# Layer 1 of a four-layer graph network: groups of 6, 7, 6, 6 blocks, a second bank for small products, and twelve blocks of features made earlier

## The chip, the cores and the metric

The kernel runs on one NeuronCore of a Trainium2 chip. A core has a matrix engine (TensorE, "PE" in the profile, with its weight loads as "PEld"), a vector engine (VectorE, DVE), a scalar engine (ScalarE, ACT), a general engine (GpSimd, POOL) and a queue that issues transfers (SyncE, SP). Each engine works through its own instructions in order and waits on semaphores for the others. Matrix products are written to PSUM, which this program uses as eight banks of 128 x 512 fp32 values. Everything else lies in SBUF or in device memory (HBM).

The metric is the time of one execution in microseconds on the device. A profile is one execution with the profiler on; its span runs from the first instruction to the last.

## What is computed

The input is a graph of 3125 nodes with 128 features each and 103125 edges, sorted by destination. Four layers follow each other, each with a residual and a normalisation over the features:

```python
edge_index = jnp.stack([src, dst])
x = _layernorm(x + _L0_gnn_ref(x, src, dst, edge_weight, ...))   # relu(A_w (x W) + b)
x = _layernorm(x + _L1_gnn_ref(x, edge_index, ...))              # attention with 4 heads
x = _layernorm(x + _L2_gnn_ref(x, Wq, Wk, Wv, Wo, edge_index))   # attention with one head
x = _layernorm(x + _L3_gnn_ref(x, edge_index, ...))              # two mean aggregations, sigmoid
```

Layer 1, where the change lies, is graph attention with four heads of 32 channels:

```python
h = (x @ W).reshape(n, HEADS, C)
a_s = jnp.einsum('nhc,hc->nh', h, att_src)
a_d = jnp.einsum('nhc,hc->nh', h, att_dst)
e = jax.nn.leaky_relu(a_s[src] + a_d[dst], NEG_SLOPE)
m = jax.ops.segment_max(e, dst, num_segments=n)
p = jnp.exp(e - m[dst])
z = jax.ops.segment_sum(p, dst, num_segments=n)
alpha = p / (z[dst] + EPS_SOFTMAX)
out = jax.ops.segment_sum(h[src] * alpha[:, :, None], dst, num_segments=n)
out = out.reshape(n, HEADS * C) + gat_bias + x @ skip_W + skip_b
# then a normalisation over the features with gain ln_g and offset ln_b
```

## The kernel before

**Dense instead of sparse.** The 3125 nodes are padded to 25 blocks of 128. At its start the kernel builds from the edge list two dense 3200 x 3200 matrices in device memory: the number of edges between each pair of nodes (`f_ctd`, in bf16), and the sum of their weights (`wd`, fp32). From then on each layer is a sum of matrix products over these.

**Layer 0** multiplies `wd` with the features (`add0`, L801). Twenty of its blocks are accumulated during the building. The last five are accumulated in a tail, a loop over 25 source blocks `i` (L1191). While PE does these, the first work of layer 1 for the finished twenty blocks is hooked into the tail: their attention scores (`scores1`, with `marks` at i = 3 to 6), the copy of the scores out of PSUM (`heads`, called in `top` at i = 7), exponentials of them (`factors`, i = 9), and the features themselves (`values`, two blocks a call, at i = 13, 16, 19 and 22, so eight blocks).

**Layer 1** uses that exp of a leaky relu is one of two products of a source factor and a destination factor, and which of them is right depends only on the sign of a_s + a_d. So for each head there is a mask of 128 sources by some destinations: the edge counts where the sign is positive, 0 elsewhere. Products of the counts and of the masks with scaled features (in three bf16 parts, `vp`) give sums for all destinations.

The work is a list of steps `items` (L1229): over the groups `IG` of destination blocks, over two passes per group (heads 0 and 1, then heads 2 and 3), over 25 source blocks `c`. A step does two things:
- `masks` (L1233), two steps ahead of their use: a transfer `ct` of counts, and for each of the two heads a mask `cm`. In four of five masks ACT makes `fm` (L1255) and DVE takes a minimum with the counts (L1256); in one of five DVE does it alone (L1249). The width of all of these is the group's: 128 columns a block. At the start of a pass a transfer `adr` brings the destinations' scores.
- `products` (L1260), three matrix products for each block of the group: one with the counts (L1266) and two with the masks (L1271). Each block of the group owns one PSUM bank through a pass.

At the end of a pass DVE reduces the banks (`sums`, L1290), POOL combines the parts (L1296 to L1299), and some steps later `quotients` divides (L1306 to L1312). After the second pass `finish1` (L1039) takes over: a normalisation, the gain, offset and residual on POOL (L1052 to L1054), a second normalisation, and then for each block a turn (`turn2`: transpose at L1014, a product with layer 2's weights at L1018). These small products, and the skip products of `skips` (L1279, added by DVE at L1280), use a PSUM bank that `bank()` hands out.

**Delays.** `later(k, f)` runs `f` k steps on (L955); `step()` does what is due. So `quotients` come 4 steps after a pass's end, `finish1` 3 steps after the second quotients, the second normalisation 5 steps after the first, and turns follow every two steps. The order within an engine is made by the framework's scheduler: it takes instructions by program order, but one that it believes ready can go ahead of one that it believes waiting. What it arranged is seen in the trace.

**Banks.** In group 0 layer 0's banks are still in use: five called acc0 to acc4, two called left0 and left1, and one called tr_sa for the small scores. Four of them (acc3, acc4, left0, left1) hold group 0's sums; acc0 and acc1 serve `values` by turns, acc1 also serves as `few`, and acc2 serves `scores1` of the last blocks, which are due at steps 3 and 5; `heads` and `factors` of those blocks come at step 7. From group 1 on there are seven banks acc1_0 to acc1_6 for sums and one bank `few` for small products. `values` of the remaining blocks are made in group 0's first pass, two blocks at a time, four steps before their use.

Of the kernel before, what the change touches and what calls it, by code (L numbers as in the profile page):

```python
# [7 lines left out]
F32 = mybir.dt.float32  # L8
# [7 lines left out]
P = 128  # L16
N = 3125
NB = 25
# [11 lines left out]
H, C = 4, 32  # L30
# [467 lines left out]
Z0 = 20  # L498
# [1 line left out]
GA = 80.0  # L500
UP = 2.0**60
GM = 40.0
IG = [(0, 4), (4, 7), (11, 7), (18, 7)]
QG = [(0, 13), (13, 12)]
LN = N - (NB - 1) * P
GT = [(0, 4), (4, 4), (8, 4), (12, 4), (16, 4), (20, 2), (22, 2), (24, 1)]
# [4 lines left out]
def fast_path(  # L511
# [4 lines left out]
    nc = tc.nc  # L516
# [50 lines left out]
    zps = zero.enter_context(tc.tile_pool(name="f_zps", bufs=1, space=PSUM))  # L567
# [164 lines left out]
    watt = cst.tile([P, 2 * H], F32, name="watt")  # L732
# [138 lines left out]
    acc0 = None  # L871
# [63 lines left out]
    def turned(ps, xT, b0, n, tag="tr"):  # L935

        t = ps.tile([P, 512], F32, name="tr", tag=tag)
        for k in range(n):
            nc.tensor.transpose(t[:, k * P : (k + 1) * P], x[:, b0 + k, :], ident)
        copy(xT[:, b0 * P : (b0 + n) * P], t[:, : n * P])  # L940
# [3 lines left out]
    xT = lp.tile([P, NP], F32, name="f_xT")  # L944
# [10 lines left out]
    def later(k, f):  # L955
        due.append((now[0] + k, f))
# [123 lines left out]
    with ExitStack() as st:  # L1080
# [29 lines left out]
        def scores1(g):  # L1110

            b0, n = GB[g]
            tag = f"acc{min(g, 2)}"
            turned(zps, xT, b0, n, tag)
            for k in range(n):
                b = b0 + k
                nc.tensor.matmul(
                    t8[:, b * 2 * H : (b + 1) * 2 * H], xT[:, b * P : (b + 1) * P], watt, start=True, stop=True
                )
            t = zps.tile([P, 512], F32, name="tr_ad", tag=tag)  # L1120
            nc.tensor.matmul(t[0:H, : n * P], watt[:, H:], xT[:, b0 * P : (b0 + n) * P], start=True, stop=True)
            ad = fp.tile([H, 512], F32, name="ad", bufs=1)
            nc.scalar.copy(ad[:, : n * P], t[0:H, : n * P])
            nc.sync.dma_start(add_[:, b0 * P : (b0 + n) * P], ad[:, : n * P])

        def heads(b0, n):

            b = slice(b0, b0 + n)
            nc.vector.tensor_copy(
                sa[:, b, :], t8[:, b0 * 2 * H : (b0 + n) * 2 * H].rearrange("p (b h) -> p b h", h=2 * H)  # L1130
            )
            nc.vector.tensor_scalar(nas[:, b], sa[:, b, 0:H], -1.0, None, OP.mult)
            nc.gpsimd.tensor_scalar(bas[:, b], sa[:, b, 0:H], UP, None, OP.mult)

# [45 lines left out]
        keep = {}  # L1180

        def top():
            heads(0, Z0)
            ex = fp.tile([P, H], F32, name="ex", bufs=1)
            nc.vector.tensor_reduce(ex, sa[:, 0:Z0, 0:H].rearrange("p b h -> p h b"), AX.X, OP.max)
            keep["d"] = highest(fp, ex, H)
# [4 lines left out]
        for i in range(NB):  # L1191
            add0(tp, i, acc1, (Z0, NB - Z0))
            if i in marks:
                marks[i]()
            if i >= 13 and i % 3 == 1:
                values(ready)
                ready += 2
        tail.close()
# [5 lines left out]
            end0(acc1[g], b0, n)  # L1204
        later(3, lambda: scores1(Z0 // 4))
        later(5, lambda: scores1(Z0 // 4 + 1))
        later(7, lambda: (heads(Z0, NB - Z0), factors(Z0, NB - Z0)))

        def in_range():

# [73 lines left out]
        def sums(acc, g, hp):  # L1284

            i0, n = IG[g]
            pool = lp if (g, hp) == (len(IG) - 1, H - 2) else sp
            nz = pool.tile([P, 7, 2, PW], F32, name="nz")[:, 0:n]
            for k in range(n):
                nc.vector.tensor_reduce(  # L1290
                    nz[:, k], acc[k][:, 0 : 2 * HW].rearrange("p (h s c) -> p h c s", s=3, c=PW), AX.X, OP.add
                )
            hi = nz[:, :, :, 0:F1]
            lo = nz[:, :, :, F1 : 2 * F1]
            fbb = [fb[:, s, i0 : i0 + n, hp : hp + 2, None].to_broadcast([P, n, 2, F1]) for s in range(2)]
            nc.gpsimd.tensor_tensor(lo, lo, fbb[1], OP.mult)  # L1296
            nc.gpsimd.tensor_tensor(hi, hi, fbb[0], OP.mult)
            nc.gpsimd.tensor_tensor(hi, hi, lo, OP.add)
            nc.gpsimd.tensor_tensor(hi, hi, self_[:, i0 : i0 + n, hp : hp + 2, :], OP.add)  # L1299
            if hp == 0:  # L1300
                nc.gpsimd.tensor_copy(deg[:, i0 : i0 + n], nz[:, :, 0, 2 * F1])
            last = pool is lp

            def quotients():
                rz = pool.tile([P, 7, 2], F32, name="rz")[:, 0:n]
                nc.vector.tensor_scalar(rz, hi[:, :, :, C], 1e-38, None, OP.max)  # L1306
                nc.vector.reciprocal(rz, rz)
                nc.gpsimd.tensor_tensor(
                    hi[:, :, :, 0:C], hi[:, :, :, 0:C], rz[:, :, :, None].to_broadcast([P, n, 2, C]), OP.mult
                )  # L1310
                rh = r[:, i0 : i0 + n, hp * C : (hp + 2) * C].rearrange("p b (h c) -> p b h c", c=C)
                nc.gpsimd.tensor_tensor(rh, rh, hi[:, :, :, 0:C], OP.add)  # L1312
                if hp == H - 2:
                    later(1 if last else 3, lambda: finish1(ends[-1], g, (1, 1) if last else (1, 5)))

            later(1 if last else 4, quotients)

        ends.append(sp)
        acc = None
        for x_, (g, hp, c) in enumerate(items):  # L1320
            i0, n = IG[g]
            if (g, hp, c) == (1, 0, 0):
                zero.close()
                ap = st.enter_context(tc.tile_pool(name="f_ap1", bufs=1, space=PSUM))
                spare.append(lambda: ap.tile([P, 512], F32, name="few"))
            if c == 0:
                if g == 0:
                    acc = [zps.tile([P, 512], F32, name="acc1", tag=f"acc{3 + k}") for k in range(2)]
                    acc += [zpp.tile([P, 512], F32, name="acc1", tag=f"left{k}") for k in range(2)]
                else:  # L1330
                    acc = [ap.tile([P, 512], F32, name=f"acc1_{k}") for k in range(n)]
            if c == (2 if g else 0) and hp == (0 if g else H - 2):
                later(0, lambda: skips(i0, i0 + n))
            if (g, hp, c) == (0, 2, 5):
                later(0, in_range)
            step()
            if g == 0 and hp == 0 and ready < NB and ready <= c + 4:
                values(ready)
                ready += 2
            for y_ in range(x_ if x_ == 0 else x_ + 2, min(x_ + 3, len(items))):  # L1340
                masks(*items[y_])
            if c < NB - 2:
                for k in range(n):
                    products(acc, g, hp, c, k)
            elif c == NB - 1:
                for k in range(n):
                    products(acc, g, hp, NB - 2, k)
                    products(acc, g, hp, NB - 1, k)
                sums(acc, g, hp)
# [397 lines left out]
```

## Time and profile before

| | us |
|---|---|
| median of 3 runs | 1522.51 (1521.67 to 1522.7) |
| profiled execution, time | 1520.03 |
| profiled execution, span | 1518.2 |
| PE busy | 1386.5 (91%) |
| PE weight loads busy | 1214.1 (80%) |
| DVE busy | 979.0 (64%) |
| ACT busy | 905.9 (60%) |
| POOL busy | 129.9 (9%) |
| first product of layer 1 | at 543.6 |
| last product of layer 1 | ends at 957.3 |

How to read it: a busy share is over the whole span, which here is a front (the matrices are built), layer 0's tail, and layers 1 to 3, each limited by something else. A row of the profile names a line of the kernel, the engine, the operation, what it writes and reads, and its shape; then busy time, the mean of one instruction in ns, and the idle time of the engine just before such instructions with what ended it. A matrix product's duration includes its way through the array, so products overlap; their pace is seen from start to start. In layer 1 a step of 7 blocks has 21 products.

### The profile page before, as it was taken

The numbers are of one execution on the slowest core, as the hardware profiler recorded it, in microseconds if no ns is written. First come the engines' busy times: TensorE is split into PE (matmuls) and PEld (weight loads), VectorE is DVE, ScalarE is ACT, GpSimd is POOL, SyncE is SP. The second block draws the span as 40 slices with busy tenths as digits, with TensorE's granted clock in tenths as the row PEclk, the third lists the DMA queues.
The fourth block names the chain that finished last, engine by engine and source line by source line (L and its number), as shares of the span: only waits on it lengthen the run. The fifth ranks groups of instructions, "written<-read, shape, count | busy, mean of one in ns | idle before, by whom it ended". The sixth has DMA issues, their size and how long they took to land. (4 is left out here: it accounts for less than half of the span.)

```text
span 1518.2 us, 35039 instructions
## 1 busy us (share of the span) xinstructions
PE 1386.5 (91%) x14762; PEld 1214.1 (80%) x14775; DVE 979.0 (64%) x1619; ACT 905.9 (60%) x1847; POOL 129.9 (9%) x163
## 2 busy tenths in 40 slices
PE   4898999999998987899989989899999999999995
PEld 3798999899898876889979979677777774458995
DVE  4999999989990489879968878544465352012006
ACT  2988887878882479878778677454465331023003
POOL 1000000000000023203212311300000000000000
PEclk9999999999999999999999999999999999999997
DMA  7378887877889633444434433332222218513541
GB/s 204 93 182 230 217 221 191 245 196 207 230 229 254 214 93 98 144 124 123 129 116 120 130 92 105 119 115 68 69 60 80 76 58 301 197 43 131 197 154 46
DMA packets 209734, 223.92 MB, mean 147 GB/s; under 512 B 72988, under 2 KB 183371, under 8 KB 209309
## 3 DMA queue, kind: packets, MB, share of 16 engines
q1 hardware_dynamic: 208780, 218.51, 49.7%
q8 instruction: 117, 1.92, 0.5%
q0 software_dynamic: 400, 1.97, 0.4%
q10 hardware_dynamic: 385, 1.11, 0.2%
q14 instruction: 52, 0.43, 0.1%
HBM read 157.19 MB, written 64.36 MB: 146 GB/s over the span
## 5 line engine op out<-in xcount | busy, mean ns | idle before, releaser
L1271 PE MATMUL acc<-vp,cm 128*128 128x198 bf16 x2500 | 343.0, 251 | 7.3 <-DVE cm L1256 4.6
L1255 ACT ACTIVATE fm<-adr,bas 128x896 bf16<-128x896 f32 (+1 forms) x320 | 286.2, 952 | 68.1 <-DVE cm L1256 63.5
L1266 PE MATMUL acc<-vp,ct 128*128 128x204 bf16 x1250 | 314.2, 255 | 9.9 <-DVE vp L1174 5.6
L1271 PEld LDWEIGHTS <-cm 128*128 128x128 bf16 x2500 | 234.9, 98 | 27.1 <-issue 10.1
L901 PE MATMUL wp<-wod,ohc 128*128 128x128 bf16 x3768 | 239.1, 219 | 7.1 <-ACT cs L906 7.1
L901 PEld LDWEIGHTS <-ohc 128*128 128x128 bf16 x3768 | 220.0, 98 | 8.2 <-issue 7.8
L1256 DVE TENSOR_TENSOR cm<-fm,ct 128x896 bf16<-128x896 bf16 (+1 forms) x320 | 198.3, 650 | 36.3 <-PE acc L1271 14.8
L860 DVE TENSOR_TENSOR wod<-ohd,w 128x4096 bf16<-128x4096 bf16 (+2 forms) x122 | 221.1, 1867 | 0.6 <-PE wp L901 0.6
L866 ACT ACTIVATE wod<-ohd,wu 128x128 bf16<-128x128 bf16 x628 | 192.8, 398 | 0.0
L1411 DVE TENSOR_TENSOR e<-e,ct 128x416 f32<-128x416 f32 (+1 forms) x175 | 108.3, 625 | 106.5 <-ACT e L1410 99.2
L1410 ACT ACTIVATE e<-s,f_nm 128x416 f32<-128x416 f32 (+1 forms) x175 | 109.6, 633 | 98.1 <-PE s L1407 91.0
L1415 PEld LDWEIGHTS acc<-self__8020,e 128*128 128x128 f32 x1250 | 148.2, 193 | 20.6 <-issue 18.8
L1415 PE MATMUL acc<-self__8020,e 128*128 128x129 f32 x1250 | 148.6, 276 | 0.6 <-DVE e L1411 0.6
L1407 PE MATMUL s<-yT,f_xT 128*128 128x416 f32 (+1 forms) x350 | 142.8, 543 | 4.6 <-ACT rt L1387 4.0
L811 PE MATMUL acc<-f_xw,cw 128*128 128x128 f32 x1000 | 120.0, 280 | 5.7 <-DMA cw<-wd 5.7
L1266 PEld LDWEIGHTS <-ct 128*128 128x128 bf16 x1250 | 122.2, 98 | 2.5 <-issue 1.5
L811 PEld LDWEIGHTS acc<-f_xw,cw 128*128 128x128 f32 x1000 | 116.4, 196 | 6.3 <-DMA cw<-wd 6.3
L912 ACT COPY ws<-wp 128x512 f32<-128x512 f32 x157 | 91.8, 585 | 48.1 <-PE wp L901 46.7
L893 PE MATMUL cp<-ohc,ohd 128*128 128x125 bf16 x1256 | 95.7, 218 | 23.5 <-ACT ws L912 19.3
L1407 PEld LDWEIGHTS s<-yT,f_xT 128*128 128x128 f32 x350 | 62.2, 191 | 55.5 <-issue 39.4
L849 DVE TENSOR_TENSOR ohd<-kd,ramp 128x4096 bf16<-128x4096 bf16 (+1 forms) x41 | 90.0, 2198 | 23.5 <-PE cp L893 23.5
L893 PEld LDWEIGHTS <-ohd 128*128 128x128 bf16 x1256 | 78.2, 98 | 28.8 <-issue 28.7
(303 smaller groups left out, 1521.3 us busy)
## 6 DMA issues: line engine op xcount, KB each, us to landing
ct<-f_ctd SPq DMA_DIRECT2D x46, 800.0 KB
wd<-ws SPq DMA_DIRECT2D x39, 896.0 KB
ct<-f_ctd SPq DMA_DIRECT2D x150, 224.0 KB
cw<-wd SPq DMA_DIRECT2D x50, 640.0 KB
f_ctd<-cs SPq DMA_DIRECT2D x20, 1000.0 KB
ct<-f_ctd SPq DMA_DIRECT2D x25, 416.0 KB
ct<-f_ctd SPq DMA_DIRECT2D x25, 365.2 KB
cw<-wd SPq DMA_DIRECT2D x25, 320.0 KB
```

Source lines behind the costliest of these rows:

```text
L811: nc.tensor.matmul(accs[j // 4][:, j % 4, :], cw[:, j - h, :], xw[:, i, :], start=False, stop=(i == NB - 1 and (j % 4 == 3 or j == n - 1)) ...
L860: tip[s] = nc.vector.tensor_tensor(packed(f, ww), packed(ohd, ww), twos(w2[s])[:, ww], OP.mult)
L866: nc.scalar.activation(wod[2][:, BW + w, :], ohd[:, BW + w, :], AF.Copy, scale=w3[:, 1, at : at + 1])
L893: nc.tensor.matmul(cp[:, j, 0:KW], ohd[:, w, :], ohc[:, w, 0:KW], start=(j == 0 and q == 0), stop=(j == 3 and q == 1), skip_group_check=True,)
L901: made = nc.tensor.matmul(wp[:, j, :], ohc[:, w, :], wod[s][:, w, :], start=(j == 0 and q == 0 and s == 0), stop=(j == 3 and q == 1 and s ...
L1255: nc.scalar.activation(f[:, : n * P], at, AF.Relu, bias=bas[:, c, h : h + 1], scale=UP)
L1256: nc.vector.tensor_tensor(m[:, : n * P], f[:, : n * P], ct[:, : n * P], OP.min)
L1266: nc.tensor.matmul(out_(F1, PW), ct[:, k * P : (k + 1) * P], vp[:, c, hp : hp + 2, :, 2 * F1 : V1], start=(c == 0), stop=False, skip_group ...
L1271: nc.tensor.matmul(out_(0, 2 * F1)[:, j], ms[j][:, k * P : (k + 1) * P], vp[:, c, hp + j, :, 0 : 2 * F1], start=False, stop=(c == NB - 1 a ...
L1407: nc.tensor.matmul(s[:, :m], xT[:, c * P : (c + 1) * P], yT[:, i0 * P + a : i0 * P + a + m], start=True, stop=True)
L1410: nc.scalar.activation(e[:, a : a + m], s[:, :m], AF.Exp, bias=nm[:, q : q + 1], scale=scale)
L1415: nc.tensor.matmul(acc[k // 3][:, (k % 3) * (P + 1) : (k % 3 + 1) * (P + 1)], es[q, c][:, k * P : (k + 1) * P], vo[:, c, 0 : P + 1], start ...
```

## The change

There are five edits.

1. The groups of destination blocks are 6, 7, 6, 6 and no more 4, 7, 7, 7. Group 0's six sums lie in acc3, acc4, acc2, tr_sa, left0 and left1.
2. For that, `scores1` of the last five blocks (`b0 >= Z0`) leaves acc2 and tr_sa: it uses acc1 for its turn and its destination scores, and a tile in acc0 for its small scores, which `heads` copies at once, in the same step. `heads` takes the tile as an argument.
3. `values` runs in layer 0's tail at every odd i from 13 to 23: six calls, twelve blocks.
4. The `quotients` of group 0, in both passes, come 7 steps after the pass's end and not 4.
5. From group 1 on, `bank()` hands out `few` alone where the group has seven banks for sums, and `few` and acc1_6 by turns where it has six.

```diff
-IG = [(0, 4), (4, 7), (11, 7), (18, 7)]
+IG = [(0, 6), (6, 7), (13, 6), (19, 6)]
...
-            tag = f"acc{min(g, 2)}"
+            tag = f"acc{min(g, 2) if b0 < Z0 else 1}"
             turned(zps, xT, b0, n, tag)
+            t, a = (t8, b0) if b0 < Z0 else (zps.tile([P, 512], F32, name="tr_s", tag="acc0"), 0)
             for k in range(n):
-                b = b0 + k
                 nc.tensor.matmul(
-                    t8[:, b * 2 * H : (b + 1) * 2 * H], xT[:, b * P : (b + 1) * P], watt, start=True, stop=True
+                    t[:, (a + k) * 2 * H : (a + k + 1) * 2 * H], xT[:, (b0 + k) * P : (b0 + k + 1) * P], watt,
+                    start=True, stop=True,
                 )
+            if b0 >= Z0:
+                heads(t, b0, n)
...
-        def heads(b0, n):
+        def heads(t, b0, n):
...
-            nc.vector.tensor_copy(
-                sa[:, b, :], t8[:, b0 * 2 * H : (b0 + n) * 2 * H].rearrange("p (b h) -> p b h", h=2 * H)
-            )
+            nc.vector.tensor_copy(sa[:, b, :], t[:, 0 : n * 2 * H].rearrange("p (b h) -> p b h", h=2 * H))
...
-            heads(0, Z0)
+            heads(t8, 0, Z0)
...
-            if i >= 13 and i % 3 == 1:
+            if i >= 13 and i % 2:
...
-        later(7, lambda: (heads(Z0, NB - Z0), factors(Z0, NB - Z0)))
+        later(7, lambda: factors(Z0, NB - Z0))
...
-            later(1 if last else 4, quotients)
+            later(1 if last else 4 if g else 7, quotients)
...
-                spare.append(lambda: ap.tile([P, 512], F32, name="few"))
+                turn = [0]
+
+                def few():
+
+                    turn[0] ^= len(acc) < 7
+                    return ap.tile([P, 512], F32, name="acc1_6" if turn[0] else "few")
+
+                spare.append(few)
...
-                    acc = [zps.tile([P, 512], F32, name="acc1", tag=f"acc{3 + k}") for k in range(2)]
-                    acc += [zpp.tile([P, 512], F32, name="acc1", tag=f"left{k}") for k in range(2)]
+                    acc = [zps.tile([P, 512], F32, name="acc1", tag=f"acc{k}") for k in (3, 4, 2)]
+                    acc += [zpp.tile([P, 512], F32, name="acc1", tag=k) for k in ("tr_sa", "left0", "left1")]
```

## The prediction

> **What bounds the kernel now.** I read the page first: TensorE (PE) is busy 91% of the 1518.2 us span, VectorE (DVE) 64%, ScalarE (ACT) 60%. These are means over four layers, so they say nothing about one stage. The list of groups of instructions by line then gave the place: L1266 and L1271, the products of layer 1, start at 543.6 us and end at 957.3 us. All that the change touches lies in these 413.7 us and in the 20 us before them. The view of busy time by windows, cut at the first product of each pass (four groups of blocks, two passes of two heads each), is the one that carries this prediction. Its columns are length, then busy us of PE, weight loads, DVE, ACT, POOL, then granted clock, DMA share, GB/s:
>
> ```profile
> 543.60:595.10 51.50, 38.98 (x351) 32.34 (x352) 48.23 (x142) 48.83 (x90) 13.43 (x25) 0.97 0.31 90
> 595.10:626.90 31.80, 27.83 (x305) 26.73 (x305) 28.63 (x69) 28.37 (x43) 5.38 (x7) 1.00 0.48 141
> 626.90:684.70 57.80, 52.77 (x552) 50.70 (x552) 43.54 (x91) 45.92 (x63) 11.71 (x11) 0.97 0.41 119
> 684.70:731.90 47.20, 46.39 (x528) 46.04 (x526) 42.12 (x62) 38.31 (x40) 11.91 (x7) 1.00 0.50 143
> 731.90:794.00 62.10, 54.18 (x558) 51.06 (x556) 49.71 (x109) 46.03 (x68) 15.24 (x10) 0.97 0.37 109
> 794.00:842.50 48.50, 47.44 (x533) 46.78 (x531) 43.42 (x64) 39.25 (x45) 11.33 (x8) 1.00 0.48 139
> 842.50:904.80 62.30, 55.64 (x557) 52.12 (x555) 50.12 (x110) 46.28 (x69) 14.77 (x10) 0.95 0.33 93
> 904.80:957.30 52.50, 48.21 (x536) 46.94 (x533) 42.42 (x64) 31.61 (x38) 10.97 (x8) 1.00 0.34 93
> ```
>
> The first two rows are group 0, with 4 blocks. There DVE and ACT fill 94% and 95% of the first pass and 90% and 89% of the second, while PE idles 12.5 and 4.0 us. The other six rows are groups of 7 blocks, and there PE is the bound (87 to 98%). So blocks are paid at DVE's and ACT's price in group 0 and at PE's price elsewhere. The groups by shape show what a block costs:
>
> ```profile
> L1255 ACT ACTIVATE fm<-adr,bas 128x896 bf16<-128x896 f32 x240 | 233.8, 1032 | 64.9 <-DVE cm L1256 60.4 <-DVE mv L993 3.4 <-DVE ms L1003 0.9
> L1256 DVE TENSOR_TENSOR cm<-fm,ct 128x896 bf16<-128x896 bf16 x240 | 165.7, 721 | 32.4 <-PE acc L1271 14.2 <-ACT fm L1255 7.8 <-DMA ct<-f_ctd 3.9
> ...
> L1249 DVE SCALAR_TENSOR_TENSOR cm<-adr,nas,ct 128x896 bf16<-128x896 f32 x60 | 74.2, 1236 | 6.7 <-PE acc L1271 6.7
> ...
> L1255 ACT ACTIVATE fm<-adr,bas 128x512 bf16<-128x512 f32 x80 | 52.4, 711 | 3.1 <-DVE cm L1256 3.0
> L1256 DVE TENSOR_TENSOR cm<-fm,ct 128x512 bf16<-128x512 bf16 x80 | 32.6, 436 | 3.9 <-DMA ct<-f_ctd 2.1 <-ACT fm L1255 1.0 <-PE acc L1271 0.6
> L1249 DVE SCALAR_TENSOR_TENSOR cm<-adr,nas,ct 128x512 bf16<-128x512 f32 x20 | 15.7, 787 | 0.7 <-PE acc L1271 0.5 <-DMA ct<-f_ctd 0.2
> ```
>
> 896 columns are 7 blocks and 512 are 4, so a block more costs (1032-711)/3 = 107 ns in an L1255, 95 ns in an L1256, 150 ns in an L1249. A pass has 40 L1255, 40 L1256 and 10 L1249. **Price of one block in one pass:** ACT 4.3 us; DVE 3.8 + 1.5 = 5.3 us; PE 6.5 us (75 matmuls; in the timeline three start every 0.26 us). A 6-block group is therefore an estimate between the two rows: per step PE 1.57, ACT 1.48, DVE 1.44 us. PE still leads, but by 6% and not by 10%.
>
> Last, PE's waits in the stage. Three lines matter:
>
> ```profile
> PE few L1279 <- DVE f_xw L1280: 10.3, 7, 3.4
> ...
> PE acc L1266 <- DVE vp L1174: 5.6, 4, 2.3
> ...
> PE few L1014 <- DVE self__8020 L1020: 4.3, 5, 1.4
> ```
>
> These are total us, times, longest. `few` is the single bank for small products: the next skip product (L1279) or turn (L1014) stands at the head of PE's in-order queue until DVE has emptied it.
>
> **The change, part by part.** The counts of mask and product instructions stay; only widths move. Each pass is priced from its row.
>
> *Two blocks more in group 0.* First pass: PE 38.98 + 13.0; DVE 48.23 + 10.6; ACT 48.83 + 8.6; and two skips more (PE 0.45, DVE 0.56). Two calls of values leave it. A call is four L1160 records (0.45 us of PE by the timeline), 2.9 us of DVE (two L1164 at 0.41, L557 0.70, L560 0.78, two L1174 at 0.29), 1.9 us of ACT (three casts at 0.62) and three POOL instructions, no DMA. Sum: PE 51.6, DVE 53.6, ACT 53.7. The row had 2.7 us beyond its busiest engine; with three engines this close I take 4.0: 57.7, so **+6.2**. Second pass: PE 27.83 + 13.0 = 40.9, DVE 28.63 + 10.6 + two more L1290 at 0.57 = 40.3, ACT 36.9; with the row's 3.2 us rest 44, **+12**. Group 0: +18.2. Its mask data grow from 1024 to 1536 bytes a row; the row's DMA share of 0.31 covers that (without cover: the 1.4 us that the first product waits for ct now, again).
>
> *Twelve blocks of features in layer 0's tail.* From 526.0 to 545.6 us DVE is busy 13.9 of 19.6 us and ACT 10.6, so the two calls (5.8 us of DVE) fit barely. They go ahead of the end0 work of the last blocks and of group 0's first masks, for which PE already waits (2.3 us for L1249). Cost between 0.9 us (only their PE work) and 5.8 us (all of DVE's): I take 3, nearer the middle, since a call's six handovers between DVE and ACT leave holes that a third call can't always fill. **+3**. If products were no longer waiting for L1174 (5.6 us now), that is inside the +6.2.
>
> *Scores of the last five blocks.* Their turn and attention products move from bank acc2 to acc1, their small scores to a tile in acc0 and heads from step 7 into steps 3 and 5: two DVE instructions (0.16 us each) and one POOL more, with the masks of two steps behind them. 0.3 us, inside the first pass's 4.0.
>
> *Quotients of group 0 three steps later.* In group 1's first pass DVE sits 3.9 us behind POOL's L1054 (bn_stats at 646.9 us), with a skip's L1280 queued behind it, so PE waits 3.37 us for `few`:
>
> ```profile
> 649.10 0.64 PE L1279 MATMUL few<-f_l_swt,f_xT 128*128 128x128 f32 x2 [3.37 <-DVE f_xw L1280]
> ```
>
> The matmuls after it run at half pace (0.54 us instead of 0.34 for a pair, until 652.6): 18 of them, 1.5 us. With norm work moved from step 7 to 10, the seven skips (steps 2 to 8) are done before. DVE's wait stays, and the same wait in groups 2 and 3 costs PE 0.9 us in the mask waits. **-4**, between 0 and -5. Two of group 0's six turns spill into the next pass, **+1.1**. Group 1: -2.9.
>
> *One block less in groups 2 and 3, and a second small bank there.* Four passes lose 6.5 us of PE, 26 in all. The bank's waits in these groups are 2.3 + 2.3 (L1279), 1.7 + 0.2 + 1.4 (L1014), 1.3 (L972) = 9.2 us. Two more cold stretches follow the 2.3 us gaps, 16 matmuls at +87 ns, 1.4 us each.
>
> Here a rule of the Trainium skill is weighed. "TensorE: Matmul & The Clock Gate" (section "HAM oscillation — how this bites in real kernels") reports that double-buffered PSUM brought its kernel no further gain, and the same page's table asks only that PE idle no more than about 3 us. By it the second bank is worth nothing for the clock here, and perhaps nothing at all. The row says otherwise:
>
> ```profile
> 740.12 0.49 PE L1279 MATMUL few<-f_l_swt,f_xT 128*128 128x128 f32 x2 [2.30 <-DVE f_xw L1280]
> ...
> 741.52 0.38 PE L1266 MATMUL acc<-vp,ct 128*128 128x204 bf16 x1
> 741.70 0.54 PE L1271 MATMUL acc<-vp,cm 128*128 128x198 bf16 x2
> ```
>
> A gap of 2.30 us was enough to halve the pace 1.4 us later. Bank worth by the rule 0, by the rows at most 9.2 + 2.8 = 12.0 us. But DVE is busy nearly without a break just there, so a PE that no longer waits for the bank meets late masks. I take half, 6 us.
>
> Then: group 2 first pass, PE 54.18 - 6.5 - 0.3 (one skip) - 0.7 (half its cold stretch) = 46.6, with 6 of the row's 7.9 us rest: 52.6, **-9.5**. Second pass 47.44 - 6.5 + 0.3 (bound2 of the first thirteen blocks now ends here) + 1.0 rest = 42.3, **-6.2**. Group 3 first pass 55.64 - 6.5 - 0.3 - 1.2 + 5.5 rest = 53.1, **-9.2**. Second pass 48.21 - 6.5 - 0.5 (one turn less) + 2.5 of 4.3 rest (the bound2 waits, 1.3 + 1.0, leave it) = 43.7, **-8.8**. Together -33.7.
>
> *Layer 2.* One L1290 less between the last product and layer 2's first work: -0.6. Group 3's normalisation, now of 6 blocks, lies beside the products of L1415 and L1407.
>
> **Sum:** 18.2 + 3 - 2.9 - 33.7 - 0.6 = -16.0 us. The profiled execution took 1520.03 us (1.8 us around its span), 2.5 us less than the median of three runs, 1522.51; I carry the difference over unchanged: profile 1504, **median 1506.5**.
>
> **Rivals.** *The removed blocks are repaid at DVE's price.* If six-block groups, at 6% margin, become DVE-bound, four passes give back 5.3 us each plus 0.57 and 0.28, some -23, and the bank nothing; quotients nothing. With +21.2 in front and -0.6: about -2.5, 1520. For it: DVE shows no idle at group starts, and after POOL's stall ACT needs from 764 to 787 us to catch up. Against: the second halves of the passes run on PE with DVE at 74%. *More gain:* bank and cold stretches in full and a tail that hides the calls: -16 - 6 - 3, some 1497. *Slower: two banks too few in group 0.* acc0 and acc1 now carry 6 skips, 7 values and 6 score tiles in the first pass, 19, where three banks carried 17; each waits for a DVE or ACT queue up to two steps (3 us) deep. The price is a `few`-like wait of up to 2.3 us each; today such waits sum to 1.4 + 0.5 us in the pass. It decides from 19 x 0.85 = 16 us of added waits; at 1.2 us each, +23 gives 1530. Against: PE has 12.5 us of idle to absorb them. That the alternation does not take place at all is unlikely: it reads the list of accumulators at each call, so it holds in groups 2 and 3; without it the bank's 6 us go, 1512.5.
>
> **How the numbers follow.** Forecast 0.60 (own range 1499 to 1514), DVE's price 0.18, more gain 0.11, slower by crowding 0.11. The bounds of the tail (0.9 to 5.8), the quotients (0 to -5) and the bank (0 to -12) make the forecast's own range. The range 1496 to 1519 leaves out the slower case and part of DVE's price. What a measurement tells from no change is 0.2%, 3 us: faster means below 1519.5. DVE's price falls on both sides: faster 0.79, same 0.09, slower 0.12.
>
> **What would show it.** Group 0's two passes near 58 and 44 us, groups 2 and 3 near 95 and 97, group 1 near 102. L1279's and L1014's waits for DVE from 14.6 us to below 8, with no PE gap over 3 us in group 1. L1255 with 768 columns near 925 ns. Wrong: if group 0 is over 110 us (look for waits of L1117, L1121, L1160, L1279), or if waits of L1271 for L1256 (4.6 us now) grow to what `few` lost.

## The result, and the profile after

The changed kernel takes 1519.32 us (median of 12 runs), the kernel before 1522.47 us beside it: ratio 0.9979, 95% interval 0.9966 to 0.9992. So 3 us were gained where 16 were forecast, and the time lies just outside the stated range.

The view of busy time by windows, cut at the first product of each pass as before, with the same columns:

```profile
548.00:605.40 57.40, 50.13 (x497) 45.45 (x498) 53.01 (x133) 55.40 (x84) 11.30 (x22) 0.94 0.39 113
605.40:650.20 44.80, 42.04 (x464) 40.93 (x464) 40.70 (x77) 37.13 (x43) 7.97 (x8) 1.00 0.46 131
650.20:710.50 60.30, 53.65 (x551) 50.40 (x551) 48.10 (x101) 45.86 (x63) 14.64 (x10) 0.97 0.38 109
710.50:760.60 50.10, 47.69 (x532) 46.87 (x531) 42.40 (x62) 39.12 (x47) 10.35 (x8) 1.00 0.46 129
760.60:817.40 56.80, 47.43 (x482) 44.42 (x480) 47.37 (x108) 41.59 (x68) 14.54 (x10) 0.94 0.36 102
817.40:862.20 44.80, 41.37 (x460) 40.41 (x458) 38.67 (x67) 35.52 (x46) 9.93 (x8) 1.00 0.45 129
862.20:916.40 54.20, 48.08 (x481) 45.09 (x480) 43.67 (x102) 41.27 (x67) 13.27 (x10) 0.94 0.34 92
916.40:957.40 41.00, 40.27 (x454) 39.65 (x451) 35.17 (x58) 27.24 (x34) 11.74 (x8) 1.00 0.37 103
```

Beside the forecast (us of the two profiled executions; a group is the sum of its two passes, each pass up to the next one's first product, the last to the last product's end, which before the change is 956.7; at 957.3 the last reduction ends):

| part | before | after | change | forecast |
|---|---|---|---|---|
| end of the build to the first product of layer 1 | 76.0 | 79.5 | +3.5 | +3 |
| group 0 (4, then 6 blocks) | 83.3 | 102.2 | +18.9 | +18.2 |
| group 1 (7 blocks) | 104.9 | 110.5 | **+5.6** | -2.9 |
| groups 2 and 3 (7, then 6 blocks each) | 224.8 | 196.7 | **-28.1** | -33.7 |
| from layer 1's last product on | 561.6 | 560.1 | -1.5 | -0.6 |
| sum | | | -1.6 | -16.0 |

The build, which no edit touches, ended at 467.6 us before and at 468.5 after, and between 466.4 and 470.7 in the runs below. One profile's whole time therefore says little about 3 us. So the experiments are compared by pass, and by the time from the build's end to the stage's end (**B**: 489.0 before, 488.9 after). Most passes are steady: group 3's second pass read 41.0 in eight of the profiles, group 1's second 50.1 in four, and groups 2 and 3 together 196.7 to 197.1 in five that have the same code there. Two are not. With the same code group 0's first pass read 57.4 to 58.9 us, and group 1's first pass 60.4, 60.2 and 58.5. So about 2 us in these two, or in B, tell nothing.

TensorE is busy 370.7 us in the stage (371.4 before). Group 0 and the tail came near what was computed, and so did the price of a mask: 926 ns for L1256 (L1255 before) at 768 columns, where 925 was expected. (The inserted lines move most line numbers of layer 1 up by one.) The gain was lost in group 1, which was to take 102 us, and in group 2: 101.6 us where 95 was computed. Group 3 took 95.1, and 97 was computed.

### The profile page after: what moved, and what is told of

Read it like the earlier page. It is cut to its first block, busy times and chain, and to the rows that moved or that the text cites. A ratio compares the mean times of both kernels' runs of the same rounds, so it can differ in the third digit from the quotient of the medians.

```text
span 1517.5 us, 35041 instructions
## 1 busy us (share of the span) xinstructions
PE 1390.6 (92%) x14775; PEld 1218.8 (80%) x14775; DVE 982.5 (65%) x1621; ACT 906.6 (60%) x1847; POOL 129.5 (9%) x164
## 4 chain that ended last, share of the span: by engine, by line
PE 71%; ACT 12%; DVE 9%; DMA 3%; issue 3%; POOL 2%; SPq 0%; ACTq 0%; DVEq 0%; POOLq 0%
PE acc L1272 9%; PE acc L1423 9%; PE wp L901 8%; PE s L1415 8%; PE acc L811 7%; PE acc L1523 7%; PE acc L1599 6%; ACT wod L866 5%; PE acc L1267 5%; DVE cm L1257 3%; PE cp L893 3%; PE left L811 2%; ACT ws L912 2%; DMA cw<-wd 1%; DVE cm L1250 1%
## 5 line engine op out<-in xcount | busy, mean ns | idle before, releaser
L1272 PE MATMUL acc<-vp,cm 128*128 128x198 bf16 x2500 | 343.4, 251 | 7.6 <-DVE cm L1257 6.6
L1256 ACT ACTIVATE fm<-adr,bas 128x768 bf16<-128x768 f32 (+1 forms) x320 | 287.1, 952 | 62.3 <-DVE cm L1257 60.5
L1272 PEld LDWEIGHTS <-cm 128*128 128x128 bf16 x2500 | 235.8, 98 | 24.5 <-DVE cm L1257 8.9
L1257 DVE TENSOR_TENSOR cm<-fm,ct 128x768 bf16<-128x768 bf16 (+1 forms) x320 | 200.5, 658 | 32.2 <-PE acc L1272 17.3
L1419 DVE TENSOR_TENSOR e<-e,ct 128x416 f32<-128x416 f32 (+1 forms) x175 | 108.1, 624 | 110.3 <-ACT e L1418 102.6
L1418 ACT ACTIVATE e<-s,f_nm 128x416 f32<-128x416 f32 (+1 forms) x175 | 109.5, 632 | 103.1 <-PE s L1415 95.8
L1423 PEld LDWEIGHTS acc<-self__8020,e 128*128 128x128 f32 x1250 | 148.2, 192 | 19.8 <-issue 18.9
```

Source lines behind the costliest of these rows:

```text
L1256: nc.scalar.activation(f[:, : n * P], at, AF.Relu, bias=bas[:, c, h : h + 1], scale=UP)
L1257: nc.vector.tensor_tensor(m[:, : n * P], f[:, : n * P], ct[:, : n * P], OP.min)
L1272: nc.tensor.matmul(out_(0, 2 * F1)[:, j], ms[j][:, k * P : (k + 1) * P], vp[:, c, hp + j, :, 0 : 2 * F1], start=False, stop=(c == NB - 1 a ...
L1423: nc.tensor.matmul(acc[k // 3][:, (k % 3) * (P + 1) : (k % 3 + 1) * (P + 1)], es[q, c][:, k * P : (k + 1) * P], vo[:, c, 0 : P + 1], start ...
```

## The experiments

All are the changed kernel with one edit, except where the kernel before is named. Ratios are to the kernel before, with 95% intervals.

### Undoing single edits

**Quotients at 4 steps.**

```diff
-            later(1 if last else 4 if g else 7, quotients)
+            later(1 if last else 4, quotients)
```

> The changed kernel with group 0's quotients 4 steps after the pass again. Group 1 takes 110.5 us in the changed kernel's profile (60.4 + 50.1), 104.9 before, and 102 was predicted. If the delay itself costs group 1 its time (theory: later turns run into ScalarE's catching up), group 1 falls to about 105 and the kernel is about 5 us faster than the changed one. If the two turns more are what costs it (rival: six turns through the one bank of a seven-block group), it stays at 109 or more, and the kernel within 2 us. If the predicted step was right (a skip no longer stuck behind VectorE's wait for GpSimd), it is about 4 us slower.

Measured: group 0 106.5 (its second pass 48.2 instead of 44.7), group 1 108.1 (60.7 + 47.4), B 489.5, ratio 0.9987 (0.9976 to 0.9997). Group 1 got 2.4 us shorter, group 0 4.3 longer. None of the three expectations holds in full; the rival (109 or more for group 1, the kernel within 2 us) comes nearest. The delay moves time between the groups and is worth about nothing in sum, and the two second passes, which are steady, show how. Here all six turns of group 0 fall into group 1's first pass, and the second takes 47.4 us; in the changed kernel the delay carries two of them over, and it takes 50.1. In group 0's second pass the delay saves 3.5 us, because here a skip's addition has to wait for GpSimd's quotients:

```profile
616.32 0.29 DVE L1281 TENSOR_TENSOR f_xw<-few,f_both 128x128 f32<-128x128 f32 x1 [1.75 <-POOL f_xw L1313]
```

This also shows what edit 4 is for. Group 0's skip products are issued one a step in steps 0 to 5 of its second pass (not in the first, where the prediction put them), and each overwrites its block of the result. With six blocks, quotients at step 4 add the sums of heads 0 and 1 before the skips of blocks 4 and 5 are written (in the trace L1313 runs at 615.35 us, these two skips at 616.32 and 617.20), and this run loses the sums for both blocks. The delay comes with six blocks.

**One bank for small products.**

```diff
-                    turn[0] ^= len(acc) < 7
+                    turn[0] = 0
```

> The changed kernel with one bank for small products in all groups. Predicted worth of the second bank: 6 us, at most 12. If so, groups 2 and 3 together go from 196.7 us to 203 or more. If its waits only turned into waits for late masks (rival), they stay within 2 us of 196.7.

Measured: groups 2 and 3 196.6 us (196.7 with two banks), B 488.5, ratio 0.9981 (0.9972 to 0.999). The next run but one, also with one bank, reads 197.2. **The second bank is worth nothing in these groups of six.** PE's waits in the two groups, first in the changed kernel, then with one bank (us in total, times, longest):

```profile
PE acc L1272 <- DVE cm L1257: 6.3, 5, 3.2
PE acc L1014 <- ACT f_x L1005: 6.0, 1, 6.0
PE few L1280 <- DVE f_xw L1281: 2.2, 3, 1.4
...
PE acc L1280 <- DVE f_xw L1281: 0.5, 1, 0.5
```

```profile
PE few L1014 <- ACT f_x L1005: 7.5, 2, 5.7
PE few L1280 <- DVE f_xw L1281: 5.7, 3, 2.2
PE acc L1272 <- DVE cm L1257: 1.8, 3, 0.9
PE few L1014 <- DVE self__8020 L1020: 1.5, 2, 0.8
```

The skip's waits for its bank (L1280) fall from 5.7 to 2.7 us, the turn's for DVE from 1.5 to none that is listed, and the waits for masks (L1272) grow from 1.8 to 6.3. Over all rows of the two answers it is 19.6 us with two banks and 20.8 with one. The total stays, so the bank was only the place where PE met engines that were late.

**Eight blocks of features in the tail.**

```diff
-            if i >= 13 and i % 2:
+            if i >= 13 and i % 3 == 1:
```

> The changed kernel with eight blocks of features in the tail again. The first product of layer 1 comes 3.5 us earlier after the build than in the changed kernel (73.8 us of tail and not 77), and group 0's first pass, 57.4 us, grows. If the work only moves (theory), by 3 to 6 us, and the kernel stays within 2 us. If group 0 can't hide it at six blocks (rival), by more than 7 us.

Measured: tail 76.9 instead of 79.5, group 0's first pass 60.4 instead of 57.4, B 489.8, ratio 0.9994 (0.9985 to 1.0004). The work only moves, as expected (the expectation counts the tail from a later point); what the early features are worth, 0.9 us of B, can't be told from nothing.

**Groups alone.** Edits 1 and 2 with the three diffs above (and so again without the sums of heads 0 and 1 of blocks 4 and 5).

> Groups of 6, 7, 6, 6 alone: quotients at 4 steps, one small bank, eight blocks in the tail. If the regrouping is repaid at VectorE's price (the rival of the prediction), this is within 3 us of the kernel before. If it carries the gain and the other edits cost, it is 5 us or more faster than before; if the other edits carry the gain, it is slower than before.

Measured: groups 108.9, 106.6, 101.9, 95.3, B 489.9, ratio 0.9994 (0.9983 to 1.0004). By its number this is the first case, but not at VectorE's price: groups 2 and 3 give back 27.6 us (23 at that price), and groups 0 and 1 spend 27.3.

### What made group 1 longer

**Without two turns.** In `turns`, blocks 4 and 5 are passed over.

```diff
-                one, two = turn2(sp, i0 + j)
-                one()
-                later(1, two)
+                if not (i0 == 0 and j > 3):
+                    one, two = turn2(sp, i0 + j)
+                    one()
+                    later(1, two)
```

(The two blocks' bounds, which nothing else writes, are set to 0.)

> The changed kernel without the turns of blocks 4 and 5, so that layer 2 reads older values for these two blocks. Group 1 then carries four turns as before, not six. Theory that the two turns more, through the one bank of a seven-block group, cost group 1 its time: it falls from 110.5 to 107 us or less, and the wait of 2.31 us in its second pass goes. Rival: the wider norm work of six blocks costs it: less than 2 us.

Measured: group 1 104.8, B 483.0, ratio 0.9954 (0.9933 to 0.9976; three runs). Group 1 is 5.7 us shorter than in the changed kernel, and the theory holds for its second pass: **there the two turns cost 3.8 us** (46.3 instead of 50.1). The other 1.9, in the first pass, are not shown to be theirs: 58.5 is also what the run with one bank takes there, which issues the same instructions in group 1 as the changed kernel. The windows of the two passes:

```profile
651.60:710.10 58.50, 52.79 (x552) 50.49 (x552) 50.31 (x101) 46.02 (x63) 15.59 (x11) 0.97 0.38 112
710.10:756.40 46.30, 46.30 (x527) 45.89 (x526) 40.81 (x60) 37.95 (x42) 8.49 (x7) 1.00 0.48 140
```

In the second pass PE is busy all 46.3 us; the changed kernel needs 50.1 there for 1.4 us more of PE work. Its timeline shows where most of the rest goes. PE's last turn waits 2.31 us, and DVE's queue has L1020, which would free the bank, behind four masks:

```profile
719.45 0.33 PE L1014 MATMUL few<-f_ident,f_x 128*128 128x128 f32 x1 [2.31 <-DVE self__8020 L1020]
```

```profile
715.61 1.97 DVE L1250 SCALAR_TENSOR_TENSOR cm<-adr,nas,ct 128x896 bf16<-128x896 f32 x1
717.51 1.68 DVE L1257 TENSOR_TENSOR cm<-fm,ct 128x896 bf16<-128x896 bf16 x3
719.11 0.28 DVE L1020 COPY self__8020<-few 128x128 f32<-128x128 f32 x1
```

This is the pass's beginning, where DVE has just reduced seven banks.

**Without all finishing work of two blocks.** `finish1` of group 0 takes blocks 0 to 3 only.

```diff
         i0, n = IG[g]
+        if g == 0:
+            n = 4
+            nc.gpsimd.memset(nq[:, 4:6], 0.0)
```

> The changed kernel in which the finishing work of group 0 (both normalisations, GpSimd's three instructions, turns) is done for blocks 0 to 3 alone, so blocks 4 and 5 go on unnormalised. Theory: group 1's first pass pays for the finishing work of group 0's two more blocks, normalisations and GpSimd as well as turns; it falls from 60.4 us to the 57.7 of the kernel before or less, its second pass to 46.3, group 1 to 103 us or less, 2 us or more below the run without the two turns (104.8). Rival: the turns alone cost it; then it stays at 104.8, within 1.5 us.

Measured: group 1 103.1, B 479.6, ratio 0.9955 (0.9937 to 0.9972):

```profile
649.90:706.60 56.70, 51.39 (x551) 49.27 (x551) 44.69 (x93) 44.36 (x59) 12.67 (x11) 1.00 0.41 116
706.60:752.90 46.30, 46.30 (x526) 45.86 (x525) 40.81 (x60) 37.95 (x42) 8.49 (x7) 1.00 0.48 140
```

It lies between: 1.7 us below the run without the turns, where 2 or more and 1.5 or less were set. The second pass is the same 46.3, so there the turns are the whole cost. The 1.7 us are all in the first pass (56.7 instead of 58.5) and within its spread: that normalisations and GpSimd for two blocks more cost anything is likely, and not shown.

**Five blocks in group 0.** Groups of 5, 7, 7, 6; tr_sa is left free.

```diff
-IG = [(0, 6), (6, 7), (13, 6), (19, 6)]
+IG = [(0, 5), (5, 7), (12, 7), (19, 6)]
...
-                    acc += [zpp.tile([P, 512], F32, name="acc1", tag=k) for k in ("tr_sa", "left0", "left1")]
+                    acc += [zpp.tile([P, 512], F32, name="acc1", tag=k) for k in ("left0", "left1")]
```

> Groups of 5, 7, 7, 6: one block moved from the last group to group 0, all other edits as in the changed kernel (the bank tr_sa is left free). If each moved block is repaid by its passes in group 0 (9.5 us) and by its finishing work in the next group (2.8 us by the 5.6 us that group 1 grew for two), group 0 takes about 93 us, group 1 about 107.5, group 2 stays at 110.6, group 3 takes about 101, and the stage is within 2 us of 411. If group 1's growth is not proportional but comes from turns that spill over a pass's start, group 1 stays within 1 us of 104.9 or at 110.

Measured: groups 90.7, 105.8, 110.6, 103.5, stage 410.6, B 489.9, ratio 0.9983 (0.9972 to 0.9995). Group 1 grew by 0.9 us for the first block handed over, then by 4.7 for the second (2.8 if the run with one bank, 108.6, is taken). Its steady second pass shows it best: 47.2 us with four turns handed over, 47.5 with five, 50.1 with six. So the cost is not proportional. Nor does a turn cost it by merely running over the pass's start: the fifth does so here, 1.9 us into the pass, and costs 0.3. It is the sixth, at 8.9 us in the changed kernel, that waits. Whether the single bank is the cause was asked of the next run.

**Groups of 6, 6, 7, 6.**

```diff
-IG = [(0, 6), (6, 7), (13, 6), (19, 6)]
+IG = [(0, 6), (6, 6), (12, 7), (19, 6)]
```

> Groups of 6, 6, 7, 6: the changed kernel with the group of seven third and not second. Group 1 then has two small banks for its six turns. If the single bank makes the turns dear there (theory), groups 1 and 2 together are 4 us or more below the changed kernel's 212.1. If VectorE's place in its queue does (rival), they stay within 2 us.

Measured: groups 102.0, 96.1, 108.5, 103.9, B 488.1, ratio 0.9985 (0.9973 to 0.9998). Groups 1 and 2 together are 204.6, 7.5 us below the changed kernel's 212.1; but group 3, which now carries seven turns, pays 8.8. Two banks and six blocks behind group 0 help there, and the time comes back two groups on: this does not decide between bank and queue. It does show what counts. A group of six that finishes six blocks of the group before takes 95.1 us (group 3 of the changed kernel) or 96.1 (group 1 here), and one that finishes seven takes 101.6 (group 2 of the changed kernel) or 103.9 (group 3 here). The seventh block's finishing work goes with 5.5 to 8.8 us, wherever it falls.

**The copy on ScalarE.**

```diff
-            nc.vector.tensor_copy(vo[:, b, 0:P], t[:, 2 * P : 3 * P])
+            nc.scalar.copy(vo[:, b, 0:P], t[:, 2 * P : 3 * P])
```

> The changed kernel with the copy at the end of a turn (L1020) on ScalarE and not VectorE. VectorE waits 5.4 us in the stage for ScalarE's L1019, which reads the same bank. If that handing over is what holds the bank (theory), TensorE's waits of L1014 for L1020 (4.8 us) fall below 2 and the stage by 3 us or more. If ScalarE's queue is as deep as VectorE's (rival), the stage stays within 2 us.

Measured: stage 411.2 (409.4), B 492.0, ratio 0.9983 (0.9973 to 0.9993). L1014's wait for L1020 falls to 2.3 us, but L1018 now waits 8.0 us for L537 and L539 (1.5 in the changed kernel). The stage stays within 2 us, so the rival holds: the bank waits as long behind ScalarE's queue.

### What DVE waits for

**Without GpSimd's part of the first normalisation.** Lines 1052 to 1054 (gain, offset, residual) are left out in all groups.

```diff
-            nc.gpsimd.tensor_tensor(rs, rs, g_row[:, None, :].to_broadcast([P, n, P]), OP.mult)
-            nc.gpsimd.tensor_tensor(rs, rs, b_row[:, None, :].to_broadcast([P, n, P]), OP.add)
-            nc.gpsimd.tensor_tensor(rs, rs, xs, OP.add)
```

> The changed kernel without layer 1's gain, offset and residual on GpSimd (three instructions a group, some 6.5 us of GpSimd for seven blocks), so its output is of another function. In the changed kernel the first passes of groups 1 to 3 take 60.4, 56.7 and 54.2 us, where the products alone need 45.9, 39.4 and 39.4. Theory: there VectorE is held up by GpSimd, by waiting for these results and by stretched instructions beside them, and TensorE's waits, whatever they are called, follow from that: the three passes lose 5 us each or more, and the waits for the small bank and for masks both shrink. Rival: it is VectorE's and ScalarE's own work at a pass's start (reductions, skips, turns): under 2 us each.

Measured: B 472.9, ratio 0.9847 (0.9823 to 0.9872; two runs only). The first passes of groups 1 to 3:

```profile
648.00:701.90 53.90, 51.08 (x552) 49.37 (x551) 46.20 (x101) 45.79 (x63) 8.15 (x7) 1.00 0.42 122
752.00:802.70 50.70, 45.89 (x480) 43.00 (x479) 44.08 (x108) 41.24 (x68) 7.89 (x7) 1.00 0.39 114
847.50:898.90 51.40, 46.62 (x482) 44.41 (x480) 42.62 (x103) 41.26 (x67) 7.16 (x7) 0.97 0.35 97
```

They lose 6.5, 6.0 and 2.9 us, the third less than the 5 that were set. The wait for masks (both lines) goes from 7.5 us to 1.6, and VectorE's 7.3 us of waiting for L1054 go. PE is busy 5.6 us less in the three passes, as fewer products run at half pace. But the waits of turns for ACT stay in sum: those of L1014 fall from 6.9 to 1.7 us, those of L1018 grow from 0.2 to 4.8. The skips' wait for their bank stays at 6.5 (6.7), and group 1's second pass at 50.1. So the theory holds for masks, and not for turns, nor for skips, which come before this work.

**Eight steps between the normalisations**, and **with two steps for their halves.**

```diff
-                    later(1 if last else 3, lambda: finish1(ends[-1], g, (1, 1) if last else (1, 5)))
+                    later(1 if last else 3, lambda: finish1(ends[-1], g, (1, 1) if last else (1, 8)))
```

> The changed kernel with 8 steps and not 5 between layer 1's first and second normalisation in groups 0 to 2. A step of six blocks is 1.58 us and not 1.84, so five steps are 7.9 us and not 9.2, while GpSimd needs 6.6 us for the seven blocks of group 1. Theory: the delay, counted in steps, is too short; with 8 the wait of 5.95 us before a turn in group 2's first pass goes, and VectorE's 7.3 us of waiting for GpSimd in the stage, and the stage is 5 to 10 us shorter. Rival: only stretched instructions matter, or the scheduler puts the second normalisation as early as before: within 2 us.

> As the one with 8 steps, and with two steps and not one between each normalisation's two halves and before the turns, in groups 0 to 2. If TensorE's waits for a turn come from ScalarE's normalisation being asked for a step too soon (theory), the waits of L1014 for L1005 (6.9 us) go entirely, and this is 2 us or more faster than the one with 8 steps alone. If VectorE's total work bounds the passes (rival), both take the same time.

Measured with (1, 8): groups 102.9, 112.3, 99.6, 95.9, B 488.8, ratio 0.9982 (0.9973 to 0.9991). The wait of 5.95 us is gone, first passes 2 and 3 are 3.3 and 1.6 us shorter, and second passes are 1.4 to 2.3 longer, for more turns fall into them. VectorE still waits 5.6 us for L1054. With (2, 8): 103.2, 112.8, 100.6, 95.6, B 490.1, ratio 0.9999 (0.9989 to 1.0009); no wait of L1014 for L1005 is left, as expected, but L1018 now waits 7.3 us for ACT. Neither brought the gain that was expected: the same time appears in another pass.

### Late turns

```diff
-            later(gap[0], lambda: turns(0))
+            later(gap[2], lambda: turns(0))
...
-                    later(1 if last else 3, lambda: finish1(ends[-1], g, (1, 1) if last else (1, 5)))
+                    later(1 if last else 3, lambda: finish1(ends[-1], g, (1, 1, 1) if last else (1, 5, 17 if g else 14)))
```

> The changed kernel with the turns of groups 0 to 2 beginning at step 31 of the next group, 6 steps into its second pass, and not at step 15 to 18. Theory: a turn is dear where VectorE is behind (around GpSimd's work and at a pass's start, where VectorE reduces the banks), and two of them spilling over a pass's start cost group 1 most of its 5.6 us; in the quiet part of the second pass, where VectorE is busy 74 to 87%, a turn costs only its own 0.65 us of TensorE. Then first passes of groups 1 to 3 lose 3 to 6 us each, second passes gain 2 to 4, and the stage is 6 us or more shorter. Rival: a turn costs 2.9 us wherever it stands: no change within 2 us.

> The kernel before with its turns late in the same way. If the regrouping's gain of some 16 us was eaten by turns alone (theory), this stays near the kernel before (within 4 us), and the changed kernel with late turns is some 10 us faster than this. If turns are as dear in both (rival), both gain the same, and the two with late turns stay within 3 us of each other.

Measured, changed kernel: B 486.1, ratio **0.997 (0.996 to 0.998)**, 1517.96 us beside 1522.94, the lowest median of a kernel that computes the whole function. Kernel before with late turns (17 for all groups): B 489.8, ratio 1.0014 (1.0006 to 1.0022). Groups 1 to 3 of the former, six passes:

```profile
651.90:708.40 56.50, 49.30 (x539) 47.59 (x539) 44.50 (x91) 44.59 (x55) 14.65 (x10) 0.99 0.41 124
708.40:762.30 53.90, 52.69 (x543) 50.65 (x543) 46.13 (x73) 39.87 (x55) 14.14 (x8) 0.95 0.38 111
762.30:814.40 52.10, 44.39 (x465) 42.07 (x463) 43.48 (x96) 39.89 (x56) 14.53 (x10) 0.97 0.38 115
814.40:862.20 47.80, 45.21 (x474) 42.57 (x474) 41.89 (x78) 37.08 (x58) 12.04 (x8) 1.00 0.41 117
862.20:910.60 48.40, 43.41 (x465) 42.13 (x464) 41.06 (x93) 37.95 (x53) 13.27 (x10) 0.96 0.38 103
910.60:956.40 45.80, 43.79 (x470) 41.84 (x468) 38.22 (x67) 30.76 (x49) 12.29 (x8) 1.00 0.33 92
```

First passes fall by 3.8, 4.7 and 5.8 us, second passes grow by 3.8, 3.0 and 4.8, so 2.8 us remain of the 6 expected. In the quiet part six turns cost group 1 some 7.6 us (53.9 instead of 46.3), 1.3 each. That is two thirds of what the two spilling ones cost (1.9 each), and twice their own PE time. Between the two kernels with late turns the ratios differ by 0.4%, some 6.7 us, where about 10 and under 3 were set (B differs by 3.7). With turns as they were, it is 3 us. So their place cost a part of the regrouping's gain, and not all of it.

**6, 6, 7, 6 with late turns.** Both diffs together.

> Groups of 6, 6, 7, 6 with late turns, the two best so far together: late turns took 2.8 us from the end of the stage, the order 6, 6, 7, 6 took 0.8. If they add, the time from the build's end to the stage's end is about 485 us and the kernel 0.3 to 0.4% faster than the kernel before; if both remove the same wait, it is as with late turns alone, 486.

Measured: groups 102.5, 97.7, 110.5, 98.4, B 488.0, ratio 0.9975 (0.9963 to 0.9986). They do not add. None of the versions is clearly faster than the changed kernel: all intervals overlap with its 0.9966 to 0.9992.

## Why the prediction was wrong, step by step

- **Tail, +3: right, with some luck** (+3.5). Over all profiles it reads 77.4 to 80.8 us with twelve blocks (median 78.1) and 76.0 to 77.3 with eight, so +1.4 is nearer.
- **Group 0, +6.2 and +12: right** (57.4 and 44.7 us where 57.7 and 44 were computed), the first pass by two misses that cancel: ScalarE is busy 55.40 us in it, 53.7 were computed, and 2.0 us are left beyond it, not 4.0.
- **Group 1's first pass, "-4" for the quotients: did not come.** It took 60.4 us (58.5 at the least) where 53.7 was computed, 57.7 before. The wait of 3.37 us did go, but the first skips now wait 2.31 + 0.69 us (1.40 + 0.22 before), behind six reductions and not four, and a turn waits 2.50 us for L1020, with 18 products at half pace behind it. The sum named what went and put nothing in its place. Even with the finishing work of four blocks, as before, the pass takes 56.7.
- **Group 1's second pass, "+1.1" for the two turns that spill: mis-sized, 3.8 measured** (50.1 and 46.3 us). The turns were priced by their own PE time, 1.4 us; the wait of 2.31 us at a single bank that DVE frees late was not in the price. It is edit 4, priced as a gain in the step before, that makes them spill.
- **Second bank, "I take half, 6 us": wrong, about 0 measured.** The step took waits named after the bank as the bank's (9.2 us; 1.1 more, in group 2's second pass, were left out). The doubt it voiced (a PE that no longer waits meets late masks) is what happened: 19.6 us of waits with two banks, 20.8 with one. Over the stage the waits of skips and turns for DVE fell from 14.6 to 12.0 us, where below 8 was set. What the Trainium skill's page "TensorE: Matmul & The Clock Gate" (section "HAM oscillation — how this bites in real kernels") reports of its kernel, no further gain from double-buffered PSUM, holds here too. The cold stretches did not go either: 18 and 29 products at half pace in groups 2 and 3, around waits of 5.95 and 3.19 us. Nor is a wait of 2.3 us always enough for one: before the change, those of 2.27 us (at 571.2), 2.49 (626.9) and 2.90 (769.8) were followed by none.
- **One block less in groups 2 and 3, 26 us at PE's price: right as a sum.** With one bank they lose 28.2, but by pass 5.7, 3.6, 8.1 and 10.8, and not 6.5 each. In the changed kernel groups 2 and 3 lose 9.0 and 19.1 us where 15.7 and 18.0 were forecast: group 2 still finishes the seven blocks of group 1, group 3 only six.
- Off the forecast: group 1 by 8.5 us (6.7 and 1.8 in its passes), groups 2 and 3 by 5.6, the other parts together by 0.3. Sum 14.4, which leads from -16.0 to -1.6.
- **Rivals.** DVE's price gave 1520 and the time is 1519.3, but by another way: it let four passes give back 23 us, and they gave 28; group 1's growth was not in it. Crowding of group 0's two banks did not happen: no wait of L1117, L1124 or L1161 is in the list of PE's waits, and the longest for L1175 is 1.5 us.

What stays open: why a turn in the quiet part costs 1.3 us and not 0.65, what lengthens group 1's first pass, and whether six turns would be as dear in group 1 with a second bank but seven blocks, which needs a ninth bank and wasn't tried.

## What to carry to other kernels

A block moved between stages takes its finishing work along, and that is paid in the stage after; price it there, at the place where it lands, with the waits that it meets. A wait on a buffer is a wait for the engine that empties it: another buffer helps only if that engine is not late anyway, and the test is whether the sum of all waits falls, not the one row. Where the waits of a stage merely change places under four different edits, look for the engine that they all lead to before tuning delays.

## What the runs showed of the hardware

VectorE's two-input masks stretch while GpSimd works. From the timelines of the changed kernel (start, length), GpSimd first, then VectorE:

```profile
784.01 2.09 POOL L1052 TENSOR_TENSOR f_xw<-f_xw,f_g_row 128x896 f32<-128x896 f32 x1 [10.50 <-ACT f_xw L1005]
786.18 2.28 POOL L1053 TENSOR_TENSOR f_xw<-f_xw,f_b_row 128x896 f32<-128x896 f32 x1
788.54 2.28 POOL L1054 TENSOR_TENSOR f_xw<-f_xw,f_x 128x896 f32<-128x896 f32 x1
```

```profile
782.48 1.02 DVE L1257 TENSOR_TENSOR cm<-fm,ct 128x768 bf16<-128x768 bf16 x2
784.73 4.14 DVE L1257 TENSOR_TENSOR cm<-fm,ct 128x768 bf16<-128x768 bf16 x2 [1.23 <-ACT fm L1256]
790.85 1.45 DVE L991 BATCH_NORM_STATS2 bs<-f_xw 128x6 f32<-128x128 f32 x7 [1.98 <-POOL f_xw L1054]
```

Two masks of 768 columns take 4.14 us beside GpSimd's instructions, where two take 1.02 us just before. One by one, they end at 786.52 and 788.88 us, 0.42 and 0.41 us after one of GpSimd's instructions (786.10 and 788.46). Taken over the stage, L1257 at 768 columns takes 551 ns on average where no GpSimd instruction overlaps it (185 of them), and 949 ns where one does (55): 22 us. Of these 55, 27 take over 0.9 us, and every one of the 27 ends 0.41 to 0.42 us after the end of a GpSimd instruction, as if it had waited for it. The mean of 642 ns, from which such a mask is priced, hides this.

The Trainium skill's page "SBUF — State Buffer" (section "SBUF: two separate sides") states it: a VectorE operation with two SBUF inputs and a GpSimd operation that reads SBUF exclude each other for a whole instruction. These ends agree. It should have been weighed before, but how much of the stage's time it explains is not shown. All masks together are stretched by 36.8 us in the changed kernel, by 33.1 in the kernel before, and by 30.1 without GpSimd's three instructions. The 15.4 us that the three first passes lost in that run come in part from this and in part from VectorE's waits for the results, such as the 1.98 us above, and the skips' waits for the small bank stayed.
